# Messages of two graph layers by seven quarter products over a pair of feature chunks

## The chip, the cores and the metric

The kernel runs on one core of one Trainium2 chip. The metric is the device time of one execution in microseconds. Engines go by the names that the profile gives them: PE is the matrix engine (PEld its weight load), DVE the vector engine, ACT the scalar engine, POOL the GpSimd engine, SP the engine whose queue issues most DMAs.

## The reference

Sixteen graphs of 1024 nodes with 128 features pass one small graph network (layer 0 below, `first_gnn` in the kernel), then one of four layers; after each of the two networks comes a residual and a layer norm. All is float32. The part that matters:

```python
def _layer(nodes, adj, ws, bs, wd, bd, wn, bn, wu, bu):
    src = nodes @ ws + bs
    src_agg = jnp.einsum('bjv,bij->biv', src, _l2norm(adj, 2))
    dst = nodes @ wd + bd
    dst_agg = jnp.einsum('bjv,bji->biv', dst, _l2norm(adj, 1))
    self_rep = nodes @ wn + bn
    upd = jnp.concatenate([src_agg, self_rep, dst_agg], axis=2)
    return jnp.tanh(upd @ wu + bu)
...
for i in range(NUM_LAYERS):
    if i < half:
        stashed.append(fpass)
    elif i == half:
        fpass = jnp.concatenate([fpass, stashed[NUM_LAYERS - i - 1]], axis=2)
    else:
        fpass = jnp.concatenate([fpass, stashed[NUM_LAYERS - i], stashed[NUM_LAYERS - i - 1]], axis=2)
    fpass = _layer(fpass, adj, *params[i])
```

So layers one and two see 128 features (one chunk), layer three 256 (two chunks: the output of layer two and that of layer one), layer four 384 (three chunks: the output of layer three, that of layer one, and the network's input).

## The kernel before, in words

The weights are folded at the start: `fold_begin` and `fold_end` multiply ws, wd and wn by the three parts of wu, so that each layer needs, per node j, two *messages* of 128 values (for the source and the destination sum) and an *own part*, and the update is tanh of (own + messages times adjacency + bias). In the code layers are numbered from 0: `l == 2` is layer three, `l == 3` layer four. V is 64, P 128, HW 512 (half of the nodes), NJ 4 (four blocks of 128 nodes, half of the nodes).

`messages(b, l, feats, wm, between)` computes the messages of a layer: for each of eight blocks of nodes and each feature chunk, `by_halves` issues two matmuls that use 64 columns of PE each (stationary: features, moving: 256 columns of weights), into one of four rotating PSUM banks (tag `pt`). After each two blocks DVE adds the bias on the way to SBUF (L650). Then DVE makes the sums S1 to S4 (L662 to L665) that a seven-product (Winograd) scheme of 2x2 quarters needs. Calls in `between` put other work behind each of the four groups.

`aggregate(...)` is the large product of messages and adjacency, by seven products on quarters (M1 to M4, Z11, Z12, Z21, each for destination and source), with the own part among them. It builds two lists of matmuls, `upper` and `lower`, for the two 64-column halves of PE, and issues them in turn, two instructions to a float32 matmul (L858). `events` and `hooks` are dictionaries from a step to the work that is issued before that step: readings of PSUM by ACT and DVE, and work for the next batch. The own part of layers three and four uses seven products too, over a *pair* of chunks (`PAIRED`): `own_sums` makes sums of the weights once, and `feature_sums` (L800 to L803) makes sums of the features, on DVE, at step 2 of layer three and step 8 of layer four. In layer three the sums of layer one's output go to a tile of their own (`fs`, in the buffer of the weights), in layer four they are written in place.

The order of all engines is that of the program (`manual_schedule`): every engine and the SP queue run their instructions in the order of issue, and wait by semaphores.

Work around the change, in each batch but the first and the last:

- End of layer two: `column_sums` of the next batch's squared adjacency, then `inverses(n, st)` (a product with `fold` on PE, three small DVE operations, a power on POOL, L328).
- In the messages of layer three: `factors` (DVE L349 to L352, which ends with the transpose `invt`; then, on SP, a DMA of it to DRAM, `dr`, and two that spread it over all partitions, `cinv`) behind the first group, and `end1_and_load` (loads of x, a norm's last product L413, its store) behind the second.
- In layer three's aggregate: `factors_of_rows` (`sp`, step 2), four calls of `scale` (sixteen DVE products L366 that multiply the next batch's adjacency by `cinv`, steps 4 to 9), `quarter1`, `x_sums`, `quarter2` (steps 12, 14, 25), and the readings of the layer's products (L731 to L749, L860).
- Then `first_gnn` of the next batch, whose last lines on PE multiply w0 by `e1` and `e0` (`pw<-e_f`, L204), which DVE finishes at L529 and L537.
- In the messages of layer four: `add0`, `spread0`, `sum0`, `centre0` behind the four groups (a layer norm: L578, L375, L382, and a product with `fold` and L389), then `squares0` at step 0 of the aggregate (`v`, L398) and `rstd0` at step 7 (a product of `fold` and `v` on PE, `pv`).

The first batch takes layer one by `plain_layer`, whose hooks hold the folding of the weights of layers three and four and the scaling by DVE (`second0` at step 11, `first0`, `sums0`); the last batch has no work of a next one.

Of the kernel before, what the change touches and what calls it, by code (L numbers as in the profile page):

```python
# [8 lines left out]
F32 = mybir.dt.float32  # L9
# [5 lines left out]
P = 128  # L15
NL = 4
CHUNKS = [1, 1, 2, 3]
G = 4
# [5 lines left out]
def adj_resnorm_kernel(ctx: ExitStack, tc: tile.TileContext, x, adj, w0, b0, layers, out):  # L24
# [33 lines left out]
    nc = tc.nc  # L58
# [34 lines left out]
    fold = const.tile([P, P], F32, name="fold")  # L93
# [5 lines left out]
    S1W, S2W, S3W, S4W, REST = V, 2 * P, 2 * P + V, 3 * P, 3 * P + V  # L99
    wx = {l: const.tile([P, REST + (CHUNKS[l] - 2) * P], F32, name=f"wx{l}") for l in PAIRED}  # L100
# [5 lines left out]
    WIDTH = [(CHUNKS[l] + 1) * 2 * P + (0 if l in PAIRED else P) for l in range(NL)]  # L106
# [3 lines left out]
    def own_weights(wm, l, c):  # L110

        if l in PAIRED:
            at = dict(zip(PAIRED[l], (0, P))).get(c, REST)
            return wx[l][:, at:at + P]
        return wm[:, CHUNKS[l] + 1, :P]

    def own_sums(l):

        def w(at):
            return wx[l][:, at:at + V]  # L120

        nc.vector.tensor_sub(w(S3W), w(0), w(S1W))
        nc.vector.tensor_add(w(S1W), w(S1W), w(P + V))
        nc.vector.tensor_sub(w(S2W), w(S1W), w(0))
        nc.vector.tensor_sub(w(S4W), w(P), w(S2W))
# [16 lines left out]
    def message_tile(name):  # L142

        return one.tile([P, 4, 2 * P], F32, tag="wm", name=name)

    def fetch_weights(raw, l, q, wm=None):
        ws, bs, wd, bd, wn, bn, wu, bu = layers[l]
        nch = CHUNKS[l]
        flat = raw.take(max(3 * nch * P, KEPT[l] * 2 * P))
# [8 lines left out]
        if wm is None:  # L158
            wm = flat[:, :KEPT[l] * 2 * P].rearrange("p (c v) -> p c v", c=KEPT[l])
        return wr, wur, bc, wm, [raw.take(3 * P).rearrange("p (k v) -> p k v", k=3) for _ in range(nch)]  # L160

    def fold_begin(l, fetched, copy=nc.scalar.copy, later=False):
# [13 lines left out]
        def biases():  # L176
            nc.scalar.copy(wm[:, 0], pm[:, :2 * P])
            nc.scalar.activation(bout[l], pm[:, 2 * P:2 * P + 1], AF.Identity, bias=bc[:, 3:4])
# [3 lines left out]
    def fold_end(l, fetched):  # L182
        _, wur, _, wm, wTs = fetched
        for c in range(CHUNKS[l]):
# [4 lines left out]
            nc.scalar.copy(wm[:, 1 + c], pm[:, :2 * P])  # L189
            nc.scalar.copy(own_weights(wm, l, c), pm[:, 2 * P:3 * P])  # L190
        nc.sync.dma_start(wsave[l], wm.rearrange("p c v -> p (c v)")[:, :WIDTH[l]])

    def message_weights(b, l):
        wm = message_tile(f"wm{l + 1}_{b}")
        nc.sync.dma_start(wm.rearrange("p c v -> p (c v)")[:, :WIDTH[l]], wsave[l])
        return wm
# [4 lines left out]
    def by_halves(out, x, y, start=True, stop=True):  # L201

        for s in (slice(V, P), slice(V)):
            nc.tensor.matmul(out[s], x[:, s], y, start=start, stop=stop)  # L204

# [108 lines left out]
    def inverses(b, state, first=0):  # L314
# [3 lines left out]
        by_halves(pc, fold, state["part"])  # L318
# [19 lines left out]
    def gather_inverses(b, spread):  # L338
        pr = small(f"rp{b}")
        by_halves(pr, fold, spread.rearrange("p h g k -> p (h g k)"))  # L340
# [44 lines left out]
    def norm_centre(ys, s, ks, name):  # L385
        n = ks.stop - ks.start
        pm = small(f"pm{name}")
        by_halves(pm[:, :n], fold, s)
# [12 lines left out]
    def norm_rstd(v, ks, name):  # L401
        n = ks.stop - ks.start
        pv = small(f"pv{name}")
        by_halves(pv[:, :n], fold, v)
# [233 lines left out]
    def messages(b, l, feats, wm, between={}, with_sums=True):  # L638
# [15 lines left out]
        if not with_sums:  # L654
            return t


# [8 lines left out]
        return X, S  # L666

# [27 lines left out]
    def aggregate(b, l, feats, msgs, wm, a, at, T, Q, fT, etag, hooks={}, pieces=1, sums=None):  # L695
# [4 lines left out]
        low, high = slice(0, V), slice(V, P)  # L700
        Z0, Z1 = (product(f"z{h}_{l}_{b}", h) for h in range(NH))

        Ck = product(f"m4_{l}_{b}")
        Dk = product(f"m3_{l}_{b}")
        A, Bk = (product(f"m{i}_{l}_{b}") for i in (1, 2))
        e0 = one.tile([P, HW], F32, tag="e0", name=f"e0_{l}_{b}")
        e12 = one.tile([P, 2, HW], F32, tag=etag, name=f"e12_{l}_{b}")
        e1, e2 = e12[:, 0], e12[:, 1]
# [84 lines left out]
        else:  # L793
            f0, f1 = (next(f for f, c in feats if c == k) for k in PAIRED[l])
            rest = [(f, c) for f, c in feats if c not in PAIRED[l]]
            y = {(j, h): f[:, half(h)] for j, f in enumerate((f0, f1)) for h in range(NH)}
            y4, y3 = (y[0, 1], y[0, 0]) if sums is None else sums

            def feature_sums():
                nc.vector.tensor_sub(y4, y[0, 1], y[0, 0])  # L800
                nc.vector.tensor_sub(y[1, 1], y[1, 1], y4)
                nc.vector.tensor_sub(y3, y[1, 1], y[0, 0])
                nc.vector.tensor_sub(y[1, 0], y[1, 0], y[1, 1])  # L803

            def w(at):
                return wx[l][:, at:at + V]

            own_of = {"M1": (w(0), y[0, 0]), "M2": (w(S2W), y[1, 1]), "M3": (w(S3W), y3), "M4": (w(S1W), y4),
                      "Z11": (w(P), y[1, 0]), "Z12": (w(S4W), y[1, 1]), "Z21": (w(P + V), y[1, 0])}

            def of_own(name, *gs):
                x, f = own_of[name]
                return [(x, blocks(f), *gs)]

            m3, m3s = prod("M3", DST), prod("M3", SRC)
            lower_m3 = of_own("M3", slice(0, G // 2)) + m3[NJ - 1:]
            upper_m3 = m3s[:NJ - 1] + of_own("M3", slice(G // 2, G)) + m3s[NJ - 1:]
            m4 = prod("M4", DST) + prod("M4", SRC) + of_own("M4")
            z12 = prod("Z12", SRC) + prod("Z12", DST)
            if l < NL - 1:  # L820
                z11 = prod("Z11", SRC) + prod("Z11", DST)
                upper = [
                    (A, True, of_own("M1") + prod("M1", DST) + prod("M1", SRC)),
                    (Bk, True, prod("M2", DST) + prod("M2", SRC) + of_own("M2")), (A, True, upper_m3),
                    (Z0, True, prod("Z21", DST) + prod("Z21", SRC) + of_own("Z21")),
# [654 lines left out]
```

## Time and profile before

| what | us |
| --- | --- |
| median of three runs | 2414.78 |
| lowest and highest | 2414.66, 2415.45 |
| the profiled execution, its own time | 2415.3 |
| span of its instructions | 2413.5 |
| PE busy | 2395.7 |
| DVE busy | 1987.1 |
| ACT busy | 955.2 |
| POOL busy | 274.0 |
| mean busy share of the 16 DMA engines, whole span | 43% |
| messages of layer four, one batch (96 instructions on PE) | 10.36 |

The profile is of one execution. A row of a timeline gives start and duration in us, engine, line of the code, operation, the tile that is written and those that are read, the shape, how many instructions are merged, and in brackets how long the engine had been idle before and who ended that. A row of the groups gives the count, the busy time, the mean duration in ns, then the idle time before them. In the view of waits a row is: who waited for whom, us in total, times, longest. Durations overlap: on PE two halves run side by side and each matmul starts before the one ahead has ended, and on DVE an instruction can start some 0.09 us before the one ahead ends.

### The profile page before, as it was taken

Reading aid. Unit: us, or ns where it says so; the run is one execution under the profiler, and the core shown is the slowest. Engines: PE = TensorE matmul, PEld = TensorE weight load, DVE = VectorE, ACT = ScalarE, POOL = GpSimd, SP = SyncE. Lnnn points to the kernel's source line nnn. Section 1 sums busy time; section 2 is a strip of 40 time slices with the busy share of each in tenths; the row PEclk is TensorE's granted clock in tenths of the full one; section 3 lists DMA queues with packets and bytes.
Section 4 is the critical chain, followed back from the end, with each engine's and each line's share of the span. In section 5 each row is a group of like instructions: output and inputs, shape, how many; then the busy total and the mean of one; then the engine's idle time right before and its main releaser. Section 6 shows DMA issues by size and latency. Waiting matters only on the chain.

```text
span 2413.5 us, 34671 instructions
## 1 busy us (share of the span) xinstructions
PE 2395.7 (99%) x13245; PEld 1034.8 (43%) x13245; DVE 1987.1 (82%) x2631; ACT 955.2 (40%) x1795; POOL 274.0 (11%) x102
## 2 busy tenths in 40 slices
PE   8999999999999999999999999999999999999998
PEld 4444344443434434344444444434444344443533
DVE  5888888898887988879788788887888888798853
ACT  5415344253342624426243351534415334262321
POOL 4101111001111011110011110111100111101100
PEclk9999999999999999999999999999999999999999
DMA  9527253362633527245272442725337263362400
GB/s 206 107 59 152 54 121 74 74 144 45 143 66 82 122 45 162 49 94 108 49 164 57 96 91 60 153 60 113 74 74 146 50 135 69 79 130 44 99 16 18
DMA packets 365732, 222.09 MB, mean 92 GB/s; under 512 B 152768, under 2 KB 336832, under 8 KB 365568
## 3 DMA queue, kind: packets, MB, share of 16 engines
q1 hardware_dynamic: 364800, 217.53, 42.3%
q0 software_dynamic: 768, 2.36, 0.4%
q8 instruction: 105, 1.72, 0.3%
q14 instruction: 59, 0.48, 0.1%
HBM read 201.20 MB, written 18.60 MB: 91 GB/s over the span
## 4 chain that ended last, share of the span: by engine, by line
PE 95%; DVE 2%; DMA 1%; SPq 1%; ACT 0%; issue 0%; POOLq 0%; DVEq 0%; ACTq 0%
PE m L858 46%; PE z L858 23%; PE pt L204 16%; PE m_f L535 5%; PE pw L204 2%; PE z_f L535 2%; DMA raw<-in_L_gnn_ws_dram 1%; PE z L692 1%; SPq L592 0%; DVE acc L283 0%; DMA rows<-in_adj_dram 0%; DMA a<-in_adj_dram 0%; PE d L692 0%; SPq L152 0%; ACT a L269 0%
## 5 line engine op out<-in xcount | busy, mean ns | idle before, releaser
L858 PE MATMUL m<-Q,S 128*64 128x512 f32 x1008 | 453.2, 593 | 0.0
L858 PE MATMUL m<-T,S 128*64 128x512 f32 x1008 | 415.4, 593 | 0.0
L408 POOL TENSOR_TENSOR rs<-ve,mhalf 128x32 f32<-128x32 f32 x30 | 191.6, 6385 | 1931.0 <-DVE ve L406 1931.0
L858 PE MATMUL m<-at,t 128*64 128x512 f32 x1008 | 409.9, 593 | 0.0
L858 PE MATMUL m<-a,t 128*64 128x512 f32 x1008 | 409.4, 593 | 0.0
L650 DVE TENSOR_TENSOR t<-pt,wm 128x512 f32<-128x512 f32 x256 | 170.8, 685 | 132.5 <-PE pt L204 132.5
L858 PEld LDWEIGHTS m<-Q,S 128*64 128x64 f32 x1008 | 135.6, 137 | 252.4 <-issue 237.6
L858 PE MATMUL z<-at,t 128*64 128x512 f32 x504 | 229.2, 592 | 0.0
L858 PE MATMUL z<-a,S 128*64 128x512 f32 x504 | 227.0, 593 | 0.0
L858 PE MATMUL z<-Q,t 128*64 128x512 f32 x504 | 226.6, 592 | 0.4 <-DVE Q L634 0.4
L858 PE MATMUL z<-a,t 128*64 128x512 f32 x504 | 226.8, 592 | 0.0
L858 PE MATMUL z<-at,S 128*64 128x512 f32 x504 | 226.7, 592 | 0.0
L204 PE MATMUL pt<-wm,f1T 128*64 128x256 f32 x1536 | 213.2, 380 | 0.0
L723 ACT COPY e<-m 64x512 f32<-64x512 f32 x63 | 36.6, 581 | 434.9 <-PE m L858 434.6
L858 PEld LDWEIGHTS m<-a,t 128*64 128x64 f32 x1008 | 126.6, 137 | 130.2 <-issue 116.6
L858 PEld LDWEIGHTS m<-at,t 128*64 128x64 f32 x1008 | 126.0, 137 | 125.2 <-issue 120.4
L858 PEld LDWEIGHTS m<-T,S 128*64 128x64 f32 x1008 | 127.1, 137 | 120.8 <-issue 115.0
L858 PE MATMUL z<-T,t 128*64 128x512 f32 x384 | 172.8, 592 | 0.0
L366 DVE TENSOR_TENSOR a<-a,cinv 128x512 f32<-128x512 f32 x250 | 154.2, 697 | 6.2 <-DMA xn<-in_x_dram 2.7
L204 PE MATMUL pt<-wm,f23T 128*64 128x256 f32 x1024 | 154.0, 379 | 0.6 <-ACT f23T L871 0.6
L274 ACT ACTIVATE sq<-a 128x1024 f32<-128x1024 f32 x120 | 125.8, 1049 | 67.5 <-DVE acc L283 63.0
L204 PE MATMUL pt<-wm,x_T 128*64 128x256 f32 x1024 | 136.1, 379 | 0.0
(260 smaller groups left out, 4420.6 us busy)
## 6 DMA issues: line engine op xcount, KB each, us to landing
a<-in_adj_dram SPq DMA_DIRECT2D x120, 512.0 KB, 12.4
rows<-in_adj_dram SPq DMA_DIRECT2D x480, 64.0 KB, 2.1
a<-in_adj_dram SPq DMA_DIRECT2D x240, 128.0 KB, 4.5
wm<-wsave SPq DMA_DIRECT2D x31, 320.0 KB, 3.5
wm<-wsave SPq DMA_DIRECT2D x16, 512.0 KB, 6.4
xn<-in_x_dram SPq DMA_DIRECT2D x124, 64.0 KB, 5.5
xs<-in_x_dram SPq DMA_DIRECT2D x60, 128.0 KB, 3.5
cinv<-dr SPq DMA_DIRECT2D x30, 256.0 KB, 6.2
```

The costliest lines, as they stand in the source:

```text
L204: nc.tensor.matmul(out[s], x[:, s], y, start=start, stop=stop)
L274: nc.scalar.activation(sq, a[:, i, :], AF.Square, accum_out=state["cols"][:, i:i + 1])
L366: engine.tensor_mul(a[:, i, s], a[:, i, s], cinv[:, s])
L408: nc.gpsimd.tensor_tensor(rstd, ve, mhalf[:, :n], ALU.pow)
L535: nc.tensor.matmul(o, x_, y_, start=start, stop=stop)
L650: nc.vector.tensor_add(t[j][:, o:o + 2].rearrange("p k a v c -> p k (a v c)"), pt, wm[:, 0][:, None, :].to_broadcast([P, 2, 2 * P]))
L692: nc.tensor.matmul(nodes(o) if len(y.shape) == 4 else o, x_, y, start=start, stop=stop)
L723: nc.scalar.copy(e0[high], A[high])
L858: nc.tensor.matmul(o, x, y_, start=start, stop=stop)
```

## The change

Layers three and four compute their messages with the seven products of the own part, instead of chunk by chunk.

- `paired_messages` takes the place of `messages` for layers three and four. The features of the pair, split in two chunks by two halves of the nodes, are the quarters; the weights of the pair, split in two chunks by two halves of the output, are the others. Seven products of 512 nodes by 128 columns (four blocks, two halves each) go to rotating PSUM banks; layer four's third chunk is added into the banks of z11, z12, z21, and into one of its own, p11. DVE adds them up into the messages, and ACT copies one.
- The sums of the features are made ahead: `y4` at step 11 of layer two's aggregate (in place, it stays for layer four), T2 in `begin_paired` (at step 27 of layer two's aggregate, and ahead of layer four's messages), T3 and T4 in `paired_messages`. The own part uses them; T2 and T4 lie in the tile of e1 and e2, T3 in that of e0. `feature_sums` goes.
- The sums of the weights, now for messages and own part, are made once in `second0` of the first batch (`sums_of_weights`), which also saves the weights; `own_sums` goes from layer two.
- The own part's products come first in `aggregate`, the last block of M3's destination part is split instead of M3's own part, and the order of the PSUM banks is another.
- `factors`, in `between`, is called where `at(0)` stands; for the first batch `inverses3` is at `at(0)` and `factors` at `at(1)`.
- The saved weights are 1408 columns wide in both layers (they were 768 and 1024). `fold` is 64 columns wide instead of 128, with the same products.

```diff
+    def weight_sums(w):
+
+        nc.vector.tensor_sub(w["S3"], w["w00"], w["S1"])
+        nc.vector.tensor_add(w["S1"], w["S1"], w["w11"])
+        nc.vector.tensor_sub(w["S2"], w["S1"], w["w00"])
+        nc.vector.tensor_sub(w["S4"], w["w01"], w["S2"])
+
+    def sums_of_weights(l, wm):
+        for w in (message_seven(wm), own_seven(l, wm)):
+            weight_sums(w)
+        nc.vector.tensor_sub(wm[:, P:2 * P], wm[:, P:2 * P], wm[:, :P])
+        nc.sync.dma_start(wsave[l], wm)
...
+    def begin_paired(b, l, first, second, etag):
+
+        e12 = one.tile([P, 2, HW], F32, tag=etag, name=f"e12_{l}_{b}")
+        y = {(j, h): f[:, half(h)] for j, f in enumerate((first, second)) for h in range(NH)}
+        w = {"e12": e12, "y": y, "T2": e12[:, 1], "T4": e12[:, 0]}
+        nc.vector.tensor_sub(w["T2"], y[1, 1], y[0, 1])
+        return w
...
+        def into(pt, *terms):
+            for i, (f, x) in enumerate(terms):
+                for k in range(NJ):
+                    by_halves(pt[:, k * P:(k + 1) * P], f[:, k * P:(k + 1) * P], x, i == k == 0,
+                              i == len(terms) - 1 and k == NJ - 1)
+            return pt
...
+        if l == 2:
+            m4 = into(bank(4), (y[0, 1], s["S1"]))
+            nc.scalar.copy(X[1, 1], parts(m4))
+            m1 = into(bank(1), (y[0, 0], s["w00"]))
+            add_bias((0, 0), parts(m1), 0)
+            t3()
+            t4()
+            z12 = into(bank("z12"), (y[1, 1], s["S4"]))
+            m2 = into(bank(2), (T2, s["S2"]))
+            add((0, 1), (0, 0), m2)
+            m3 = into(bank(3), (T3, s["S3"]))
+            add((1, 0), (0, 1), m3)
+            add_sbuf((0, 1), (1, 1))
+            add((0, 1), (0, 1), z12)
+            z11 = into(bank("z11"), (y[1, 0], s["w01"]))
+            add((0, 0), (0, 0), z11)
+            z21 = into(small(f"pt{l + 1}_{b}_z21", [HW]), (T4, s["w11"]))
+            at(0)
+            add_bias((1, 0), X[1, 0], 1)
+            add_sbuf((1, 1), (1, 0))
+            add((1, 0), (1, 0), z21)
+        else:
+            t4()
+            t3()
+            m4 = into(bank(4), (y[0, 1], s["S1"]))
+            nc.scalar.copy(X[1, 1], parts(m4))
+            at(0)
+            m1 = into(bank(1), (y[0, 0], s["w00"]))
+            add_bias((0, 0), parts(m1), 0)
+            at(1)
+            z11 = into(bank("z11"), (y[1, 0], s["w01"]), *plain(0, 0))
+            at(2)
+            z12 = into(bank("z12"), (y[1, 1], s["S4"]), *plain(0, 1))
+            m2 = into(bank(2), (T2, s["S2"]))
+            add((0, 1), (0, 0), m2)
+            add((0, 0), (0, 0), z11)
+            at(3)
+            m3 = into(bank(3), (T3, s["S3"]))
+            add((1, 0), (0, 1), m3)
+            add_bias((1, 0), X[1, 0], 1)
+            add_sbuf((0, 1), (1, 1))
+            add((0, 1), (0, 1), z12)
+            add_sbuf((1, 1), (1, 0))
+            z21 = into(small(f"pt{l + 1}_{b}_z21", [HW]), (T4, s["w11"]), *plain(1, 0))
+            add((1, 0), (1, 0), z21)
+            p11 = into(bank("p11"), *plain(1, 1))
+            add((1, 1), (1, 1), p11)
+        XS = message_sums(b, l, t)
+        if l == 2:
+            at(1)
+        return XS
...
-            def feature_sums():
-                nc.vector.tensor_sub(y4, y[0, 1], y[0, 0])
-                nc.vector.tensor_sub(y[1, 1], y[1, 1], y4)
-                nc.vector.tensor_sub(y3, y[1, 1], y[0, 0])
-                nc.vector.tensor_sub(y[1, 0], y[1, 0], y[1, 1])
...
+            own_upper = [(Z0, l == 2, own_of["Z21"]), (A, True, own_of["M1"]), (Bk, True, own_of["M2"])]
+            own_lower = [(Z1, l == 2, own_of["Z12"]), (Z0, l == 2, own_of["Z11"]), (Dk, True, own_of["M3"])]
...
             def second0(destination, finish):
                 columns0(range(NJ, NB), 1)
+                for l in PAIRED:
+                    sums_of_weights(l, fetched[l][3])
                 destination(1, cinv[0])
                 columns0(range(NJ), 1)
...
-                     8: folded(2, fold_end), 9: lambda *_: fold_and_scale(3, 0), 11: second0, 12: folded(3, fold_end),
+                     8: folded(2, fold_end), 9: lambda *_: fold_and_scale(3, 0), 10: folded(3, fold_end), 11: second0,
...
-        if b == 0:
-            hooks = alongside(hooks, {9: lambda: own_sums(2), 12: lambda: own_sums(3)})
+        p = {}
+
+        def y4(f=f1):
+            nc.vector.tensor_sub(f[:, half(1)], f[:, half(1)], f[:, half(0)])
+
+        def t2(p=p, f1=f1, f2=f23, b=b):
+            p.update(begin_paired(b, 2, f1, f2, "acc"))
+
+        hooks = alongside(hooks, {11: y4, 27: t2})
...
-                between = {1: inverses3, 3: factors}
+                between = {0: inverses3, 1: factors}
...
-        t = messages(b, 2, feats, wm, between)
-        sums = message_tile(f"fs_{b}").rearrange("p c v -> p (c v)")
+        t = paired_messages(b, 2, p, wm, None, between)
...
-        t = messages(b, 3, feats, wm, between)
+        p = begin_paired(b, 3, f1, x1T, "row")
+        t = paired_messages(b, 3, p, wm, f23, between)
```

## The prediction

> **What bounds the kernel now.** I read the page first (engine shares), then the groups by shape, then the timeline of one middle batch (556 to 630 us, batch 3), then the list of waits.
>
> ```profile
> PE 2395.7 (99%) x13245; PEld 1034.8 (43%) x13245; DVE 1987.1 (82%) x2631; ACT 955.2 (40%) x1795; POOL 274.0 (11%) x102
> ...
> L650 DVE TENSOR_TENSOR t<-pt,wm 128x512 f32<-128x512 f32 x256 | 170.8, 685 | 132.5 <-PE pt L204 132.5
> ```
>
> PE is the bound: 99% busy, at granted clock 1.00. The reader is to see the second number too: DVE at 82% works in a fixed order beside it, so what counts is where DVE is late, not its average. A batch takes 147.7 us (in the chain of waits the messages of layer four begin at 312.54, 460.24, 607.95).
>
> The price of message matmuls is their pitch, from the PE timeline:
>
> ```profile
> 32.96 0.83 PE L187 MATMUL wm<-raw 128*128 128x128 f32 x6
> ...
> 608.64 0.60 PE L204 MATMUL pt<-wm,f23T 128*64 128x256 f32 x4
> 609.07 0.60 PE L204 MATMUL pt<-wm,x_T 128*64 128x256 f32 x4
> ```
>
> Every f32 matmul is two instructions, and the two 64-column halves run side by side: a group of four (two pairs) of 256 columns starts every 0.43 us, 0.216 a pair; a pair of 512 columns takes 0.429. The price is linear in columns. For 128 columns the nearest row is L187: six full-width matmuls, mean 275 ns, in 0.83 us, so (0.83 - 0.275) / 5 = 0.111; the line through the two pairs gives 0.109. I take 0.110 for a pair.
>
> **What the matmuls save.** Layer three before: 8 blocks x 2 chunks x 2 pairs = 32 pairs of 256, 6.9 us (558.24 to 565.17). After: 7 products x 4 blocks x 2 = 56 pairs of 128, 6.16 us: -0.77. Layer four: 48 pairs of 256, 10.36 us, become 56 + 4 x 8 = 88 pairs of 128, 9.68 us: -0.68. Together -1.45 a batch, -23 us in 16. The own part has as many matmuls as before. Bounds: 0.107 a pair (256 halved twice), and 0.137 (the duration of one 64-column weight load, if two loads no longer hid).
>
> [...]
>
> **What DVE is given.** DVE prices: 0.69 us for a 128x512 add; the next starts 0.60 after it if independent (the 16 scalings of L366), 0.72 if it needs the result (L663 to L664). Layer three had 4 adds and 4 feature sums; now 9 adds and T3, T4 (y4 and T2 move into layer two, into idle time: DVE waits 1.23 us before the last add there). Layer four had 4 adds and 4 sums after the messages; now 10 adds, and T2, T4, T3 ahead of them. One ACT copy (0.6) a layer is hidden, ACT is idle.
>
> Where DVE stood in layer three:
>
> ```profile
> 563.13 0.21 DVE L352 STREAM_TRANSPOSE invt<-inv 128x32 f32<-128x32 f32 x1
> ...
> 571.85 0.18 DVE L333 TENSOR_TENSOR sp<-inv,group 128x32 f32<-128x32 f32 x1
> 572.23 3.10 DVE L366 TENSOR_TENSOR a<-a,cinv 128x512 f32<-128x512 f32 x5 [0.19 <-DMA cinv<-dr]
> ```
>
> The reader is to see that `factors` (which ends with invt) starts a chain of two DMAs whose landing, 8.5 to 8.9 us later, is just when DVE gets to the scalings. Before, `factors` came after the first message add, held up only by POOL's power (inv, done 562.65). The change puts it after z11. Working DVE through from the layer's first matmul at 558.24: m1 is done at 560.2, add_bias(0,0) 560.2, T3 560.8, T4 561.4, add of m2 (done 562.0) 562.0, m3 562.8, add_sbuf 563.4, z12 564.15, z11 564.75, `factors` 565.35 to 566.0. So invt ends 2.65 us later (563.34 to 566.0), cinv lands at 574.5 to 574.9, and DVE, which after the remaining three adds, five sums, the norm and sp arrives at 572.2, idles 2.4 us. On SP's queue the loads of xn and the store of y follow cinv and come 2.65 us later with it; xn landed at 574.2 and is needed at 584.2, so that costs nothing. In PE's queue nothing waits in this stretch: X(0,0) is ready at 565.4, needed at 564.4 + 3 x 0.858 = 567.0; S3 at 568.5, needed 568.7.
>
> Behind that wait DVE has 34 us with hardly a gap (16 scalings, combine, sums, transposes, T2 to T4, the first GNN's reads), to the point where PE needs it:
>
> ```profile
> 605.52 0.69 DVE L537 TENSOR_TENSOR e_f<-e_f,dinv 128x512 f32<-128x512 f32 x1
> ```
>
> It ends 606.21; PE uses it (second half of the pw<-e_f group that starts at 606.06) at 606.92: 0.7 us of slack, and 0.31 more in one wait of DVE for PE. That this slack is all is seen in batch 1, where cinv came late by itself:
>
> ```profile
> 267.17 0.21 DVE L352 STREAM_TRANSPOSE invt<-inv 128x32 f32<-128x32 f32 x1
> ...
> 277.69 2.50 DVE L366 TENSOR_TENSOR a<-a,cinv 128x512 f32<-128x512 f32 x4 [1.60 <-DMA cinv<-dr]
> ```
>
> ```profile
> 311.46 1.08 PE L204 MATMUL pw<-e_f,w0T 128*64 128x512 f32 x4 [0.28 <-DVE e_f L537]
> ```
>
> Scalings 1.42 us later against invt than in batch 3 (10.31 for 8.89) made PE start 0.44 late. After the change they are 2.4 to 2.65 late and PE is 0.77 early. L537 ends 606.21 + 2.4 - 0.31 = 608.3, up to 608.5; PE starts at 608.4 what it started at 606.92. **Layer three: +1.45 us** instead of -0.77. Bounds: +0.8 (0.6 us of small gaps close) to +2.1 (cinv as late as in batch 1 now and then).
>
> **Layer four**, from its own first matmul S (607.78 before):
>
> ```profile
> 618.36 0.69 DVE L650 TENSOR_TENSOR t<-pt,wm 128x512 f32<-128x512 f32 x1 [0.77 <-PE pt L204]
> ...
> 622.94 1.21 DVE L398 TENSOR_REDUCE v<-sq 128x32 f32<-128x1024 f32 x1
> ```
>
> ```profile
> PEld pv L204 <- DVE v L398: 9.2, 15, 0.6
> ```
>
> v is finished at 624.15 and PE takes it at 624.26 (hook 7), S + 16.48, with no time over: the weight load waits for it in all 15 batches. After: product m2 ends at S + 56 x 0.110 + 0.2 = S + 6.4 (m4, m1, and z11, z12 with two terms each go first). Behind it DVE has adds of m2 and z11, L389, m3, bias, add_sbuf, z12, add_sbuf, z21, p11, then S3 twice, S1, S2, S4, and v: 0.60 + 0.60 + 1.13 + 0.72 + 0.60 + 0.72 + 0.60 + 0.60 + 0.60 + 0.72 + 0.33 + 0.45 + 0.72 + 0.72 + 0.60 + 1.21 = 10.9. So v is at S + 17.3, PE goes on at S + 17.4 where it could at S + 9.7 + 7 x 0.858 = 15.8 (on the way M4 waits some 0.7 for S1). **+0.9 us.** Bounds: 0 (if L389 slides into DVE's 1.2 us wait for m2) to +1.7. Then DVE no longer has the four feature sums (2.8 us at 626.9), so the lateness ends here.
>
> **The ends.** Batch 0: the weight sums (18 small ones, some 5 us by L122's 0.22 and L662's 0.42) now stand in layer one ahead of `destination(1)`, and the second half waits for ACT's weight copies, which lie behind eight row scalings until 63.2; destination moves from 58.45 to about 65.8. DVE has 2.2 us of gaps until finish(0), and PE needs f1: +4.7 net of the removed own_sums. There `inverses3` comes after all products, so `factors` waits for the pool's 2.9 us: invt some 5.5 later, with no slack (PE already waits 0.76 and 0.28 for e_f there): +5. With layer four +0.9. I take +10, bounds +2 and +14. Batch 15 has no next batch and keeps its gain: -1.3. On SP's queue the two weight saves of layers three and four now stand behind these sums, until about 66 for 63; behind them layer two's weights (landed 66.94, needed 81.4) and the next batch's rows (first used 83.2, landed 78.25) move by 3 to 5 us, at the same rate as f1: nothing more. The larger weight loads (704 KB for 384 and 512) are issued over 20 us ahead, against 6.4 to landing for 512 KB: nothing.
>
> **Sum.** 14 x (1.45 + 0.9) = 33; + 10 - 1.3 = +42. The profiled execution took 2415.3 (span 2413.5 and 1.8 around it), the median is 2414.8: **2456 us**.
>
> **Rivals.**
> *The adds are hidden* and the matmuls' gain comes through: 2415 - 23 = 2392. For it: DVE waits 4.37 + 0.70 + 0.75 + 0.77 us for PE in layer four and 1.79 for POOL in layer three. Against: these waits lie ahead of the late points. It decides if the scalings shift by less than 0.98 - 0.77 = 0.2 us and v by less than 0; I find 2.4 and 0.9. Chance 0.11.
> *Narrow pairs cost a weight load, 0.137*: layer three still waits for DVE (+1.45), layer four's m2 ends 1.5 later (+2.4): 14 x 3.85 + 12 + 2.4 = +68, 2483. For it: twice the loads per column; against: L187. 0.06.
> *The lateness goes on* into the next batch (POOL's power of 7.34 us starts later, and the norm behind it): 1 to 2 us more a batch, 2470 to 2484. Against: the removed sums. 0.08.
> *Half of it*: one of the two late points is covered, +0.5 to +1.2 a batch: 2420 to 2432. 0.10. *A tie*, both points nearly covered: 0.04; there the change does less work and nobody sees it.
> My forecast, both points late: 0.61, with its own range 2432 to 2472.
>
> **How the numbers follow.** The time is that of the forecast. The range 2424 to 2480 takes in the bounds of the sum (14 x 0.8 + 2 - 1.6 = +12 to 14 x 3.8 + 14 = +67) short of their ends, leaving out the 0.11, the tie and the far end. What differs by more than 0.2% (5 us) can be told from no change: faster 0.11, same 0.04, slower 0.85.
>
> **What would show it.** In the changed kernel: pairs of 128 columns 0.11 apart; DVE waiting over 2 us for cinv in most batches; PE waiting for e_f (L536/L537's successors) and for v, near 2 and 1.6 us a batch; no PE wait in batch 15. I am wrong if invt ends within 1 us of where it did against the layer's start, or if DVE's gaps after the scalings close without PE waiting.

## The result, and the profile after

| | us |
| --- | --- |
| before, median of five runs beside it (lowest, highest) | 2414.78 (2414.66, 2416.84) |
| after, median of five runs (lowest, highest) | 2506.76 (2504.93, 2508.05) |
| after / before, 95% interval | 1.0379 (1.0364 to 1.0394) |
| span of the profiled execution, before and after | 2413.5, 2506.3 |

The change makes the kernel 92 us slower. The forecast was 2456, so the direction was right and the loss was more than twice what was forecast. First the head of the page of the changed kernel:

```profile
span 2506.3 us, 38945 instructions
## 1 busy us (share of the span) xinstructions
PE 2441.0 (97%) x15293; PEld 1191.8 (48%) x15293; DVE 2093.9 (84%) x2799; ACT 973.5 (39%) x1827; POOL 275.2 (11%) x102
```

PE fell from 99% to 97%, and DVE has 107 us more to do (2093.9 for 1987.1). PE's busy time even rose (2441.0 for 2395.7) while it had less to do, so the gain of the change can't be read from it. It is read from the pitch, in the PE timeline of a middle batch (batch 2, counted from 0; layer three):

```profile
435.82 1.95 PE L247 MATMUL pt<-wm,f1T 128*64 128x128 f32 x32
...
441.09 1.04 PE L247 MATMUL pt_z<-wm,e 128*64 128x128 f32 x16
441.97 0.59 PE L997 MATMUL z<-e,wm 128*64 128x512 f32 x1
```

The messages take 435.82 to 441.97, 6.15 us for 56 pairs: 0.110 a pair, as taken. What was lost again is in the view of waits (who waited for whom, us in total, times, longest):

```profile
DVE y L461 <- POOL inv L309: 74.5, 14, 5.3
...
DVE T L680 <- PE m L997: 39.2, 15, 2.6
...
DVE a L414 <- DMA cinv<-dr: 24.3, 10, 3.5
...
PEld m L997 <- DVE t L698: 24.0, 15, 1.6
...
PE pw L247 <- DVE e_f L577: 11.8, 15, 0.8
...
PE m L997 <- DVE t L698: 10.8, 15, 0.7
...
PE pv L252 <- DVE v L446: 8.8, 15, 0.6
...
PE pw L247 <- DVE e_f L585: 4.1, 15, 0.3
```

PE now waits for DVE at three places in each batch: e_f (first GNN), v (layer four), and t (the messages of layer *one* of the next batch, L698). The forecast has the first two, near 2 and 1.6 us a batch; by PE's own rows they are 1.1 and 0.6. The third is new, and beside it stands a wait of the other direction that before has nowhere: DVE for PE at T<-T,a, up to 2.6 us, in all 15 batches.

The most useful table is made from the PE timeline of each run: the distance between the first message product of one layer and that of the next, as the median of the middle batches (us). Layer two to layer three is 29.56 in every run, and the table leaves it out.

| kernel | layer three to four | four to one | one to two | start of layer four in batch 0 | total |
| --- | --- | --- | --- | --- | --- |
| before | 49.54 | 39.35 | 29.25 | 164.12 | 2414.8 |
| after | 51.35 | 40.46 | 31.63 | 181.48 | 2506.8 |
| t3_later | 51.32 | 40.46 | **29.21** | 180.18 | 2469.2 |
| t3_read_early | 51.28 | 40.46 | **29.91** | 179.28 | 2481.4 |
| factors_early | **48.84** | 40.47 | 31.63 | 179.42 | 2473.8 |
| rstd_later | 51.38 | **38.85** | 32.42 | 181.47 | 2494.8 |
| sums_pool | 51.21 | 40.46 | 31.63 | **172.65** | 2498.1 |
| four_fixes | 48.81 | 38.86 | 31.40 | 171.47 | 2438.3 |
| five_fixes | 48.76 | 38.87 | 31.40 | 168.34 | 2433.7 |
| seven_fixes | 48.75 | 38.87 | 30.00 | 169.60 | 2414.4 |
| seven_v | 48.75 | 38.87 | 30.00 | 168.89 | 2415.1 |
| steady | 48.75 | 38.88 | 30.00 | 165.69 | **2408.8** |
| steady_first | 48.75 | 38.88 | 30.00 | 167.70 | 2409.7 |
| gap_used | 48.75 | 38.88 | 30.60 | 166.27 | 2416.7 |

Before and after: 14 x 1.8 (layer three) + 15 x 1.1 (layer four) + 15 x 2.4 (layer one) + 17.4 (batch 0) - 1.5 (last batch) = 93.6, against 92.8 of span. That is the whole loss, by place.

The column on batch 0 scatters by some 2 us of its own: of the 17.4, 2.4 stand ahead of layer one, which begins at 39.21 after and at 36.83 before. In three profiled executions (after, rstd_later, steady_first) PE was granted a clock of 0.50 for 3.4 us between 14 and 19 us, and layer one begins at 38.5 to 39.2; in the other eleven it begins at 36.2 to 37.7.

### The profile page after: what moved, and what is told of

Read it like the earlier page. It is cut to its first block, busy times and chain, and to the rows that moved or that the text cites. A ratio compares the mean times of both kernels' runs of the same rounds, so it can differ in the third digit from the quotient of the medians.

```text
span 2506.3 us, 38945 instructions
## 1 busy us (share of the span) xinstructions
PE 2441.0 (97%) x15293; PEld 1191.8 (48%) x15293; DVE 2093.9 (84%) x2799; ACT 973.5 (39%) x1827; POOL 275.2 (11%) x102
## 3 DMA queue, kind: packets, MB, share of 16 engines
q0 software_dynamic: 768, 2.36, 0.4%
## 4 chain that ended last, share of the span: by engine, by line
PE 63%; DVE 16%; DMA 12%; SPq 5%; issue 3%; ACT 1%; DVEq 0%; POOLq 0%
PE m L997 31%; PE z L997 16%; PE pt L247 7%; PE pt_z L247 4%; DMA a<-in_adj_dram 4%; SPq L640 4%; DVE a L414 2%; DVE at L655 2%; PE m_f L583 2%; DMA kept<-y 2%; DMA xk<-kept 1%; DMA rows<-in_adj_dram 1%; PE z_f L583 1%; DVE t L698 1%; DVE f L536 1%
## 5 line engine op out<-in xcount | busy, mean ns | idle before, releaser
L997 PE MATMUL m<-T,S 128*64 128x512 f32 (+1 forms) x1072 | 435.6, 568 | 1.2
L997 PE MATMUL m<-a,t 128*64 128x512 f32 x1008 | 417.1, 596 | 11.0 <-DVE t L698 10.8
L997 PE MATMUL m<-at,t 128*64 128x512 f32 x1008 | 425.4, 595 | 0.0
L997 PEld LDWEIGHTS m<-T,S 128*64 128x64 f32 x1072 | 136.1, 137 | 137.0 <-issue 117.2
L997 PEld LDWEIGHTS m<-a,t 128*64 128x64 f32 x1008 | 119.9, 137 | 166.1 <-issue 129.0
L889 ACT COPY e<-e 64x512 f32<-64x512 f32 x63 | 38.9, 617 | 256.8 <-DVE e L888 256.8
L997 PEld LDWEIGHTS z<-Q,t 128*64 128x64 f32 x504 | 69.1, 137 | 122.0 <-issue 112.3
L247 PE MATMUL pt<-wm,f1T 128*64 128x128 f32 (+1 forms) x1536 | 122.3, 312 | 4.4 <-ACT f1T L1010 4.4
L317 ACT ACTIVATE a<-a 128x1024 f32<-128x1024 f32 x120 | 124.9, 1042 | 0.0
```

The costliest lines, as they stand in the source:

```text
L317: nc.scalar.activation(a[:, i, :], a[:, i, :], AF.Copy, accum_out=degree)
L889: nc.scalar.copy(e1[low], e0[high])
L997: nc.tensor.matmul(o, x, y_, start=start, stop=stop)
```

## The experiments

**Four edits, one for each late point** (a place where PE or DVE now stands and did not before), each alone on the changed kernel.

*t3_later*: where the new wait comes from. T[2] to T[4] are sums of quarters of the adjacency, which PE reads as a matmul's weights; `combine(i, ...)` makes T[i] on DVE. In layer four DVE makes the next batch's T[3] in place of the old one:

```diff
@ quarters0 (step 18)
-                for i in (2, 3):
-                    combine(i, y2, w["T"])
+                combine(2, y2, w["T"])
@ rows1 (step 23), at its end
+                combine(3, y2, w["T"])
```

> Only change against the changed kernel: in quarters0 (step 18 of layer four's aggregate) the next batch's combine(3) is taken out and issued on DVE at the end of rows1 (step 23) instead. Theory A (in layer four DVE must wait 2.6 us there until PE has read the old T[3] for the last time, because a half of M3's destination block is now read late; everything DVE does behind it, up to layer one's message adds, is late by that): the wait of T<-T,a for PE (39.2 us in 15 batches) falls under 5 us, PE's wait for the message adds of layer one (10.8 + 24.0 us) nearly goes, from layer four's messages to the next layer three's 101.65 becomes about 99.3, the total 2507 - 15 x 2.4 = 2471. Theory B (DVE simply has too much work in this stretch, the wait only stands where the queue is held up anyway): the wait moves to another instruction and the total stays within 8 us of 2507.

Measured: 2469.16 (1.0227 of before, 1.0212 to 1.0243), 37.6 less than after, as Theory A has it; layer one back to 29.21; the wait is gone from the list. The view of one tile on PE says why it was there. All of PE's readings of T in layer four of one batch, after (the layer begins at 488.27):

```profile
L997 PE MATMUL m<-T,S x18: 379/592/593, 507.7 to 520.8; 128*64 128x512 f32 x14, 128*64 128x256 f32 x4
...
who waited for it (us, times):
  DVE T L680: 2.6, 1
```

and before (the layer begins at 607.78):

```profile
L858 PE MATMUL m<-T,S x16: 592/592/592, 627.8 to 633.0; 128*64 128x512 f32 x16
```

The last reading starts 32.5 us into the layer, where before it was 25.2: the change splits M3's last destination block, which reads T[3], and puts one half near the end; before, the own part was split there, which reads f1T. The DVE timeline of after shows the price, with the idle time before an instruction and its releaser in brackets:

```profile
513.87 1.23 DVE L461 TENSOR_TENSOR y<-y,rs 128x1024 f32<-128x1024 f32 x1 [5.32 <-POOL inv L309]
...
516.36 2.25 DVE L678 TENSOR_TENSOR T<-a 128x2048 f32<-128x2048 f32 x1
521.22 2.29 DVE L680 TENSOR_TENSOR T<-T,a 128x2048 f32<-128x2048 f32 x1 [2.61 <-PE m L997]
```

In before the same instruction (L632) followed the one ahead of it without a wait. In t3_later it runs behind the transposes, and nothing waits:

```profile
510.69 2.25 DVE L678 TENSOR_TENSOR T<-a 128x2048 f32<-128x2048 f32 x1
...
515.06 2.37 DVE L655 STREAM_TRANSPOSE at<-a 128x1024 f32<-128x1024 f32 x2
517.36 2.25 DVE L680 TENSOR_TENSOR T<-T,a 128x2048 f32<-128x2048 f32 x1
```

*t3_read_early* is the other half of the proof: DVE's order is left alone, and PE reads T[3] two blocks earlier.

```diff
-            upper_m3, lower_m3 = m3s[:-1] + shared[1:] + m3s[-1:], shared[:1] + m3[-2:-1]
+            upper_m3, lower_m3 = m3s[:1] + shared[1:] + m3s[1:], shared[:1] + m3[-2:-1]
```

> Only change against the changed kernel: on PE, in the aggregates of layers three and four, the half block of M3's destination part goes to the second place of the upper half's M3 group instead of the last but one; DVE's order is untouched. Theory A (what DVE waits for is PE's last reading of T[3]): two blocks earlier is 2 x 0.857 = 1.7 us earlier, so T<-T,a waits 0.9 us for 2.6, and layer one's stretch (31.63 us to layer two's messages, 29.25 before the change) becomes 29.9 to 30.2, the total 2507 - 15 x 1.5 = 2484. Theory B (moving DVE's work helped in the run before because it came behind the transposes, not because of T[3]'s reader): no change, 2503 to 2510.

Measured: 2481.39, layer one 29.91, and in the DVE timeline

```profile
513.62 2.29 DVE L680 TENSOR_TENSOR T<-T,a 128x2048 f32<-128x2048 f32 x1 [0.89 <-PE m L997]
```

The wait shrinks by 1.72 us, what two blocks take on PE, and layer one by as much. So it is T[3]'s last reader, and nothing else in that stretch.

*factors_early*:

```diff
@ paired_messages, l == 2
             add((0, 1), (0, 0), m2)
+            if b:
+                at(0)
             m3 = into(bank(3), (T3, s["S3"]))
...
-            at(0)
+            if not b:
+                at(0)
             add_bias((1, 0), X[1, 0], 1)
```

> Only change against the changed kernel: in layer three's messages of all batches but the first, factors (three small DVE operations, and the DMAs to dr and cinv) is issued behind the add of m2 instead of behind z11. Theory A (the late cinv makes DVE's scalings late, and with them e_f, for which PE waits before layer four): the scalings' wait for cinv falls from 3.5 to about 0.9 us a batch, PE's waits for e_f (11.8 + 4.1 us) to under 5, from layer three's messages to layer four's 51.3 becomes about 49.2, the total 2507 - 14 x 2.1 = 2478. Theory B (the eleven adds and sums that DVE now has in this layer are what is late, whatever cinv does): cinv's wait falls, but DVE reaches e_f no earlier than now less 0.5 us, and the total is 2500 or more.

Measured: 2473.77, 33.0 less. Batch 2 before the edit, and with it:

```profile
443.59 0.21 DVE L400 STREAM_TRANSPOSE invt<-inv 128x32 f32<-128x32 f32 x1
...
453.60 1.90 DVE L414 TENSOR_TENSOR a<-a,cinv 128x512 f32<-128x512 f32 x3 [3.49 <-DMA cinv<-dr]
```

```profile
436.39 0.21 DVE L400 STREAM_TRANSPOSE invt<-inv 128x32 f32<-128x32 f32 x1
...
446.12 4.30 DVE L414 TENSOR_TENSOR a<-a,cinv 128x512 f32<-128x512 f32 x7 [0.50 <-DMA xn<-in_x_dram]
```

With the layer starting at 435.82 and 431.50, invt begins 7.8 and 4.9 us in and the scalings 17.8 and 14.6: 2.9 us earlier at the first and 3.2 at the second. PE's waits for e_f fall from 15.9 us to 2.5, and layer three to four is 48.84, which is 0.7 under before: the narrow matmuls' gain (0.77 worked out) comes through whole once cinv is in time.

*rstd_later*: `hooks = {0: squares0, 9: rstd0, 10: rows0, ...}` for 7.

> Only change against the changed kernel: rstd0 (the product pv of fold and v on PE, and combine(4)) is issued at step 9 of layer four's aggregate instead of step 7. Theory A (PE stands at pv for DVE's v, S + 17.5 for 16.4 before, and this is a delay of its own): PE passes step 7 some 1.0 us earlier, and as the late T[3] follows PE, the gain stays: total 2507 - 15 x 1.0 = 2491. Theory B (the power on POOL and the end of the norm behind it, for which DVE already waits 5.3 us, get later by the same amount and hold up the next stretch): no gain, 2503 to 2512.

Measured: 2494.75, 12.0 less. Four to one falls by 1.6, more than expected, but layer one grows by 0.8: Theory A for the most part, with a piece of B. It is the piece that comes back below.

*sums_pool*: `nc.gpsimd` for `nc.vector` in `weight_sums` and in the subtraction of `sums_of_weights`.

> Only change against the changed kernel: the eighteen sums of weights of the first batch (in second0) are made on POOL instead of DVE. Theory A (these some 5 us on DVE make the first batch's outputs of layer one late, PE then stands 4.6 us and runs at granted clock 0.50 for the next 4 us): the stall at the start of layer two's messages (4.56 us) goes under 1.5 us, its slow stretch with it, the start of layer four's messages in the first batch comes at 172 to 176 for 181.5, the total 2498 to 2502. Theory B (what is late in batch 0 is ACT's copies of the weights and the later power in layer three, not these sums): the total within 4 us of 2507, the stall before layer two's messages stays above 3 us.

Measured: 2498.12, 8.6 less; layer four of batch 0 begins 8.8 earlier (2.6 of it ahead of layer one, which the edit does not touch), and the stall in the middle of layer two's messages, 4.41 us in after, is 0.68 us:

```profile
82.90 1.95 PE L247 MATMUL pt<-wm,f1T 128*64 128x256 f32 x16
85.52 1.95 PE L247 MATMUL pt<-wm,f1T 128*64 128x256 f32 x16 [0.68 <-ACT f1T L1010]
```

The four gains alone are 37.6 + 33.0 + 12.0 + 8.6 = 91.2, as much as the whole loss of 92.0.

**Together they are not their sum.**

> The four single edits (combine(3) later, factors behind the add of m2, rstd0 at step 9, weight sums on POOL) in one kernel. Theory A (four separate late points, nothing else late): layer three to layer four 48.8, layer four to layer one 38.9 and layer one 29.3, layer two 29.56, so 146.5 a batch for 147.7 before the change; with batch 0 still some 8 us behind and the last batch 1.5 ahead 2415 - 14 x 1.2 + 8 - 1.5 = 2405 (2398 to 2412), faster than both. Theory B (they cover each other: DVE is the bound of the batch and some of the waits come back elsewhere): 2415 to 2430.

Measured: 2438.27, a miss for both theories; 91.2 less would be 2415.6. The table has the reason: layer one is 31.40, though its own fix is in. Taking v two steps later had made POOL's power, and the norm's end behind it, later too (y<-y,rs begins 26.50 us into layer four for 25.60, and the layer is 1.6 us shorter); alone that was mostly hidden, since DVE had to stand 2.6 us for T[3] behind it anyway. Without that wait it is paid in full: 31.40 against 29.21 in t3_later, 2.2 us a batch, of which the single run showed 0.8. The other 1.4 x 15 = 21 us take 2415.6 to 2437. So beside t3_later's edit, rstd0 at step 9 brings 1.6 us in layer four and costs 2.2 in layer one. No run has these two edits alone, but factors_early and sums_pool leave layer one at 31.63, as after has it. The DVE timeline of four_fixes, layer four:

```profile
488.40 2.28 DVE L682 TENSOR_TENSOR T_again<-a,T 128x2048 f32<-128x2048 f32 x1
496.00 1.23 DVE L461 TENSOR_TENSOR y<-y,rs 128x1024 f32<-128x1024 f32 x1 [5.32 <-POOL inv L309]
...
498.49 2.25 DVE L678 TENSOR_TENSOR T<-a 128x2048 f32<-128x2048 f32 x1
```

From 496.00 on DVE works for 38 us with one wait of 0.68, and 5.32 us ahead of that it has nothing to do.

*five_fixes* adds `at(0)` behind the add of m2 in batch 0 too (inverses3 there), and its factors, `at(1)`, ahead of z21's bias.

> As four_fixes, and in the first batch inverses3 is issued behind the add of m2 and factors ahead of the bias of z21's part, each one place earlier. Theory A (batch 0 is late in layer three because the power on POOL starts after all products): its stretch from layer three's to layer four's messages goes from 59 to 54 to 56 us, the total 3 to 5 us under four_fixes (about 2401). Theory B (that stretch is set by the scalings' amount, not by when they start): within 1.5 us of four_fixes.

Measured: 2433.66, 4.6 less, with that stretch of batch 0 at 53.7: Theory A.

*seven_fixes* puts the idle time to use:

```diff
             def end0(w=w):
+                w["T"] = combined(n, "T")
+                combine(2, y2, w["T"])
                 norm_end(w["ys"], w["r"], KS)
@ hooks of batch 0, layer one
-  10: folded(3, fold_end), 11: second0, 14: lambda *_: scale_rows(rows[1], 1, rinv)
+  11: second0, 13: folded(3, fold_end), 14: sums_and_rows1
```

The function `sums_and_rows1` makes the weight sums on POOL, which stood in `second0`, and then the scaling that stood at step 14.

> As five_fixes, and two more edits. (1) In layer four DVE makes the next batch's combine(2) ahead of the norm's end (in end0, step 14) and not behind it (quarters0, step 18): in four_fixes DVE stood idle 5.3 us there waiting for POOL's power, with 2.25 us of this work right behind it. (2) In batch 0 fold_end of layer four's weights goes from step 10 to step 13 of layer one, and the weight sums on POOL to step 14, so that PE does not stand 2.1 us at step 10 for ACT's copies. Theory A (after rstd0 at step 9 what is late in layer one is DVE behind POOL's power: everything from the norm's end to layer one's message adds): layer one falls from 31.4 to 29.3 to 29.6, a batch to 146.4, so 2434 - 15 x 1.9 - 2 = 2403 (2398 to 2408), faster than before the change. Theory B (DVE has no time left in this stretch whatever the order): layer one stays above 30.8, the total above 2424.

Measured: 2414.37 (0.9997, 0.9987 to 1.0006), no difference from before, and a total between the two theories. Layer one falls to 30.00, most of what was expected, but not to 29.3; and batch 0 loses 1.3 against five_fixes (0.6 of it ahead of layer one) where 2 were to be gained: with fold_end later, POOL's scalings of the adjacency begin at 68.0 for 66.8 and DVE waits for them, and PE waits 3.3 us in the middle of layer two's messages.

*seven_v*: `squares0` between S1 and S2 in `message_sums`, rstd0 at step 8.

> As seven_fixes, but v is made earlier instead of taken later: DVE makes it between S1 and S2 of layer four's messages (before: behind S4), 1.4 us earlier, and rstd0 goes to step 8 for step 9. Theory A (any hook that v makes without PE standing is as good, and the power then ends earlier, which layer one no longer needs): within 4 us of seven_fixes. Theory B (layer one still hangs on POOL's power): 5 to 15 us faster than seven_fixes. Theory C (S2 and S4 1.2 us later make PE wait for M2 and Z12): slower by over 5 us.

Measured: 2415.07 (1.0001, 0.9991 to 1.0010): Theory A, it makes no difference once combine(2) fills the time that POOL's power takes.

*steady* (without the edit of fold_end):

```diff
@ aggregate, layer four
-                    (A, False, m1), (Bk, False, m2), (A, True, upper_m3),
+                    (A, False, m1[:NJ]), (Bk, False, m2[:NJ]), (A, False, m1[NJ:]), (Bk, False, m2[NJ:]),
+                    (A, True, upper_m3),
...
-  13: m1_read, 16: m4_read, 18: m3_half, 21: m2_and_half_of_m3
+  16: m4_read, 17: m1_read, 18: m3_half, 21: m2_read, 24: half_of_m3
@ factor_row
-        for h in range(NH):
+        for h in reversed(range(NH)):
```

> As seven_v, with the batch-0 edit of fold_end taken back (weight sums on POOL in second0 again), and three edits for the other batches: in layer four's aggregate M2's destination part goes ahead of M1's source part on PE (T[2] is then read for the last time 3.4 us earlier, so that DVE, which stood 4.55 us there, makes combine(2) while POOL's power still runs); the addition that waits 0.68 us for ACT's copy goes behind the transposes; and factor_row loads cinv's second half first, which the scalings use first. Theory A (in seven_v DVE works without a gap from the norm's end to layer one's reads, 38.8 us, and layer one's 30.0 us for 29.25 hang on the 0.75 us that it is late): layer one comes to 29.25 to 29.4, a batch to 146.3 to 146.7, total 2415 - 15 x 0.75 - 14 x 0.2 - 1.5 = 2399 (2394 to 2405). Theory B (the 0.75 us come from PE itself, its two halves out of step in layer one): layer one stays at 30.0 and the total at 2408 to 2415.

Measured: 2408.80 (0.9977, 0.9968 to 0.9987): 0.2% under before, little, but the interval leaves out 1. It did not come by the step expected: layer one stays at 30.00, as Theory B has it. Of the 6.3 us under seven_v 3.2 are batch 0's (layer four begins at 165.69 for 168.89), and some 2.5 come from layer three to four, on average 48.79 for 48.97 in 14 batches, where of the edits only the order of cinv's halves lies: no batch takes over 49.07 there, where seven_v had one of 50.4. (The two later runs with that order have a mean of 48.77, the five without it whose `factors` are early 48.97 to 49.10.) Theory B's reason is at most a part: one half of PE does begin layer one 0.37 us behind the other, in t3_later 0.01, but then PE also stands for DVE twice, 0.37 us each, first for the transposes of the rows and then for Q. Q in steady, whose layer one begins at 646.12:

```profile
663.42 2.29 DVE L678 TENSOR_TENSOR Q<-at 128x2048 f32<-128x2048 f32 x1
...
665.77 0.64 PE L1004 MATMUL m<-Q,S 128*64 128x512 f32 x1
```

and in t3_later, whose layer one begins at 673.43 and takes 29.21:

```profile
689.95 2.29 DVE L678 TENSOR_TENSOR Q<-at 128x2048 f32<-128x2048 f32 x1
...
692.34 0.60 PE L997 MATMUL m<-Q,S 128*64 128x512 f32 x1
```

Q is ready 19.6 us into the layer for 18.8, and its first matmul starts at 19.65 for 18.91. The list of waits can't tell the two apart: the weight loads' wait for Q is 9.9 us in all in steady, 10.1 in t3_later and 10.3 in before.

*steady_first*: batch 0 with the sums of layer four's weights on DVE between its two pairs of transposes, layer three's on POOL, fold_end at step 13.

> As steady, and in batch 0: the sums of layer four's weights are made by DVE between its two pairs of transposes (where it stood 2.5 us waiting for ACT), those of layer three's by POOL, whose scalings of the next batch start 7 us earlier; fold_end of layer four's weights at step 13 for 10. Theory A (the stall of 2.1 us at step 10 and the half clock behind it go, and POOL's scalings are no longer late for DVE): layer two's messages start at 81.5 to 82.5 for 85.1 in five_fixes and go through without a stall over 1.5 us, total 2 to 5 us under steady. Theory B (as in seven_fixes, PE only gets to the next stall earlier): within 1.5 us of steady.

Measured: 2409.67 (0.9979, 0.9970 to 0.9988), within 1.5 us of steady: Theory B.

*gap_used* goes after the two stalls: `half_of_m3` back to step 21, combine(3) to the start of rows1, and the edit of t3_read_early.

> As steady, but the addition that waits for ACT's copy goes back to its old place (step 21), ahead of the transposes, where DVE now stands 1.69 us waiting for the rows anyway; and combine(3) stands ahead of the transposes of rows1, with PE's last reading of T[3] two blocks earlier as in t3_read_early. Theory A (layer one's missing 0.75 us are two stalls of PE, 0.37 each, behind DVE's transposes of the rows and behind its Q, at the end of a DVE chain without gaps that begins where that wait ends): DVE is 0.7 to 0.9 us earlier from there on, layer one comes to 29.25 to 29.4, total 2409 - 15 x 0.7 = 2398 (2395 to 2402). Theory B (transposes that stand 2.3 us later hold up something else, the next scalings on ACT or the norm's load): layer one stays at 30.0 or above, total 2408 or more.

Measured: 2416.73, 7.9 more than steady; a miss. ACT's order was overlooked. The two engines in gap_used, ACT first:

```profile
489.68 3.30 ACT L647 ACTIVATE a<-a,rinv 128x256 f32<-128x256 f32 x8
493.01 0.62 ACT L893 COPY e<-e 64x512 f32<-64x512 f32 x1
```

```profile
493.66 0.69 DVE L910 TENSOR_TENSOR e<-e,e 64x512 f32<-64x512 f32 x1 [2.35 <-ACT e L893]
```

The copy for which the addition waits stands behind eight scalings of rows. In steady that time was covered by the transposes. The remaining 0.75 us of layer one stay: PE's two stalls show that they hang on DVE's chain, but no version run here removes them.

## Why the prediction was half right

- **The matmuls**: right. 0.110 us a pair measured. The gain itself shows where nothing is late behind it: the last batch is 0.79 + 0.72 = 1.5 us shorter (1.3 forecast), and layer three with cinv in time 0.7. With the instructions of both halves counted one starts every 55 ns (6.15 us / 56 pairs / 2 instructions), and every 110 on each half, as in L187's row over the whole array (0.111 us), so the row was to be trusted.
- **Layer three**: right in mechanism, a little small: +1.8 for +1.45. invt ended 8.0 us into the layer (443.80 - 435.82) where the forecast had 7.8 (566.0 - 558.24), and factors_early shows that the late cinv was the cause. The wait was sized right too: 2.4 us forecast, 2.4 in the median of 14 batches (2.0 to 3.5; batch 2, shown above, is the longest). What was small is the shift of the scalings, put at that same 2.4. It was taken from batch 3 of before, where they begin 14.0 us into the layer; the median there is 13.7, and after it is 16.7, so they are 3.0 us later. That is more than the missing 0.35.
- **Layer four**: right: PE takes v at S + 17.54 for 17.4, +1.1 for +0.9.
- **"Then DVE no longer has the four feature sums (2.8 us at 626.9), so the lateness ends here"**: this step failed. The sums did go, but all that they left was idle time: the wait for POOL's power grew from 36.5 us (at most 2.6) to 74.5 (5.3). And behind the power came a wait that was never looked for. The diff's one line on M3's split was read as "as many matmuls as before"; that it also moves the last reading of T[3] by 7.3 us, and that DVE overwrites this buffer there, was in the code and in the trace of before. It cost 2.4 us a batch, 36 in all, of the 51 that the forecast of 2456 lacks; t3_later and t3_read_early show it from both sides. Of the rivals, the adds are not hidden and a narrow pair does not cost 0.137. The one that the lateness goes on into the next batch had the right place and nearly the right size (1 to 2 us), but another cause: POOL's power. In t3_later that wait is unchanged (74.4 us) and layer one is whole again.
- **Batch 0**: the mechanism was right, the term too small: +17.4 for +10, past its bound of +14, and still +15.0 from layer one's own start. Of its two pieces the +5 (the power, inverses3 and factors) was right: +4.8 from layer three to layer four, and five_fixes takes 4.9 off (58.6 to 53.7). The other, +4.7 for the weight sums on DVE, was mis-sized: +10.1 from layer one to layer three (84.79 us for 74.65), and sums_pool comes back to 76.46. The sums took 6.6 us for the 5 taken, as two of those that ran beside POOL's scalings took 1.1 and 1.3 us for 0.22; DVE waited 4.1 us for ACT's copies among them, and PE stood 4.4 us behind the chain. A piece that the sum did not have at all is PE's clock, below: behind these stalls PE ran at a granted clock of 0.50 for 3.4 + 6.8 = 10 us.

## What to carry to other kernels

When a change moves a read, ask who overwrites that buffer next: a matmul that only changes its place in the list can hold up another engine a layer later (2.4 us a batch here). A wait that hides another makes single gains add up wrongly (91.2 us one by one, 68.5 together), so the fixes are to be run together before the rest is believed. Where an engine is idle ahead of a long chain without gaps, work of that chain that does not need the awaited result belongs ahead of the wait (combine(2) brought 1.4 us a batch), but only after the orders of all engines that feed it are followed (gap_used).

## What was not expected of the hardware

**The granted clock halved behind short pauses of PE (1.9 to 4.4 us in after), for one or two times 3.41 us.** Windows of the changed kernel's batch 0 (busy us of PE, PEld, DVE, ACT, POOL, then the granted clock, DMA share, GB/s):

```profile
62.00:64.00 2.00, 0.13 (x2) 0.00 (x0) 0.00 (x0) 2.00 (x7) 0.00 (x0) 1.00 0.80 314
65.20:68.80 3.60, 3.60 (x6) 1.47 (x5) 3.07 (x7) 3.54 (x10) 2.15 (x2) 0.53 0.00 0
92.60:99.60 7.00, 6.04 (x24) 2.72 (x26) 4.25 (x9) 6.81 (x13) 0.00 (x0) 0.51 1.08 133
164.20:167.80 3.60, 3.60 (x10) 1.19 (x8) 3.56 (x6) 0.61 (x1) 0.00 (x0) 0.53 0.38 148
```

Behind the pauses of 1.9, 4.4 and 3.1 us (PE's idle time by the profile) PE has a granted clock of 0.50 from 65.34 to 68.75, from 92.64 to 99.47 and from 164.32 to 167.74, so for 3.41, 6.83 and 3.41 us: a matmul of 512 columns over the whole array then starts 0.85 us after the one ahead for 0.43. A fourth dip lies ahead of these, from 14.14 to 17.55, behind a pause of 2.98 us. The distances between the four beginnings, 51.20, 27.30 and 71.68, are 15, 8 and 21 times 3.41. So in this trace the clock changed only at the borders of windows of 3.41 us, on a grid that did not move with the pauses.

What went with a fall is how much of one window is idle. The same pause of 1.9 us (PE at L229, for ACT) was followed by a dip in three kernels (after, t3_later, five_fixes) and by none in the seven others that have it. Windows cut on each trace's own grid tell them apart: after, and then sums_pool, whose clock did not fall here.

```profile
61.92:65.33 3.41, 1.50 (x10) 1.07 (x10) 0.29 (x1) 2.82 (x11) 0.00 (x0) 1.00 0.57 221
```

```profile
57.44:60.85 3.41, 2.07 (x14) 1.50 (x12) 2.64 (x5) 3.41 (x10) 1.37 (x5) 1.00 0.73 235
60.85:64.27 3.42, 2.84 (x11) 1.73 (x12) 2.83 (x3) 2.83 (x11) 1.66 (x4) 1.00 0.23 89
```

In after the whole pause lies in one window, 1.91 us idle of 3.41; in sums_pool a border cuts it into 1.34 and 0.58. It is whole in all three kernels with a dip, and cut in all seven without (at most 1.66 in one window). Over all 14 traces, each without its last 9 us, each of the 20 falls of the clock follows a window with 1.91 us or more idle; of some 9,900 windows behind which full clock stayed, none has more than 1.94. In after the falls of batch 0 follow 2.88, 1.91, 3.41 and 2.19 us idle. That a window's idle time is what decides is inferred from these counts; no run changed it alone.

In steady it was two pauses, of 1.2 and 1.0 us, of which 1.97 us lie in one window, that a dip followed. A dip of 3.41 us costs some 1.7 us, an estimate (half of it, at a clock of 0.50); in after there are four stretches of it in batch 0, one in the last 4 us of the run, and none between, where no window has more than 1.1 us idle.

**POOL's and DVE's scalings took longer side by side.** In five_fixes, batch 0, DVE's scalings alone and beside POOL's:

```profile
59.37 2.58 DVE L414 TENSOR_TENSOR a<-a,cinv 128x512 f32<-128x512 f32 x4
...
72.12 3.10 DVE L414 TENSOR_TENSOR a<-a,cinv 128x512 f32<-128x512 f32 x2
```

```profile
66.83 7.84 POOL L414 TENSOR_TENSOR a<-a,cinv 128x512 f32<-128x512 f32 x6
```

DVE's take 0.65 us each, and 1.55 each while POOL makes the same product. Of POOL's six, the first five take 1.26 to 1.27 us and the last, beside DVE's second, 1.72; where in after three of each run side by side, DVE's take 1.75 and POOL's 1.71. Not all of DVE's work did: in five_fixes its two transposes beside POOL's scalings took 2.37 us, and two without them 2.36. What the two engines contend for is not shown. So work given to POOL was not free for DVE here; in sums_pool it mostly was, since of the 7.5 us of its sums only 2.7 fell beside work of DVE.
